# Causal products of a slot-attention kernel in blocks of 64 tokens instead of 128

## The chip, the cores and the metric

The kernel runs on one core of a Trainium2 chip. The time is the device time of one execution in microseconds. A core has five engines with a queue of their own each: TensorE (PE, with its weight loads listed as PEld), VectorE (DVE), ScalarE (ACT), GpSimd (POOL) and SyncE (SP, which here only starts DMAs). Each works through its queue in order, and semaphores make one wait for another. TensorE writes to PSUM, and ScalarE and VectorE take the results from there to SBUF.

## The reference, cut to what matters

Four sequences of 512 tokens, 512 wide, go through a layer norm, an attention with 64 slots per head, a second layer norm and a feed-forward part. The change touches the attention alone. It has 16 heads; q, k and s are 64 wide, v is 128 wide. In short, for each head:

```
z = cumlogsumexp(s) over the tokens
hk[t] = hk[t-1] * exp(z[t-1] - z[t]) + k[t] (x) exp(s[t] - z[t])     # 64 x 64
pv[t] = softmax(scale * q[t] . hk[t])                                # 64 slots
hv[t] = hv[t-1] * exp(z[t-1] - z[t]) + exp(s[t] - z[t]) (x) v[t]     # 64 x 128
o[t]  = pv[t] . hv[t]
```

With e = exp(s) and 1/z' as the inverse of e's running sum, both recurrences become sums over the past: the score of slot m at time t is (sum over u <= t of (q[t].k[u]) e[u,m]) / z'[t,m], and the output is the sum over u <= t of ((pv[t]/z'[t]) . e[u]) v[u]. Then o is normalised per head, multiplied by a weight and by silu of a gate, and projected by Wo.

## The kernel before, in words

A unit of work is a pair of heads (g, 8 of them) of one sequence (b, 4 of them): 32 units, in the order g over two sequences, then g over the other two. Keys, queries and e of the two heads lie on the two halves of the 128 partitions, transposed (feature by token). The 512 tokens are cut into NT = 4 blocks of 128. Sums over the past are done in two parts: products within a block, with a triangular mask, and products with a state, the sum over all earlier blocks. All these products are in float32. The projections are in float32r.

The parts of a unit that the change touches, with the lines of the profile:

- `diagonal_blocks` (from L607) makes, for each block and head, a 128x128 product out of 64 rows (L622), and VectorE multiplies it by the mask `tri` (L626, 128x512 per head). It is called by `query_key` (ps_a, from kT and qT) and `weight_slot` (ps_b, from eT and the weights wT).
- `states` (L636) makes the contributions of the first three blocks to the state of each head; `add_up` (L647, L649) has VectorE add them up in one copy and two adds. `key_states` calls it for keys and e (ps_sk, 64 wide), and GpSimd then copies the result into `sk_both` (L713), where both heads stand on a diagonal of 128x128; `value_states` calls it for e and v (ps_sv, 128 wide).
- `slot_scores` adds state times query (L724) and e times the masked product (L731) in one PSUM bank, and VectorE multiplies by 1/z' (okT, L739).
- `softmax` turns okT (ps_okn, L604), takes the maximum (mx, L746) and subtracts it (ok, L748); `softmax_exp` is on ScalarE (L753); `slot_weights` turns the result back (ps_w) and multiplies by 1/z' (wT, L770).
- `read_states` (L784) and `read_within` (L797) add the two parts of the output in PSUM (ps_ov). ScalarE squares it (L807), VectorE sums the squares (L808), and GpSimd raises to the power -0.5 (L812).

The order of all instructions is written out by hand in `attention`, engine by engine in program order; nothing reorders it. The output projection of the unit before (`before.project_output`, L883) is cut into pieces that stand between the steps of this unit's softmax: two of its matmuls before `softmax`, the rest of its first 128 tokens after it, and so on. Its results use the three buffers of the pool `ps3`, main and mixed part one each. ScalarE takes the main part (y, L895), and `add_output` has VectorE subtract the mixed part (L900) and GpSimd start a DMA that adds y to `stream` in memory (L901). So the third piece, `project_output(2, count=2)`, needs a buffer that `add_output(0)` releases. Ahead of `slot_scores` stand `gate_silu` for both heads (L839) and `exp_and_log`, which loads ScalarE's function table (L904).

Units with even g also project the values of two pairs of heads (L587); units with odd g do not. `other`, `piece`, `small` and `next_step` put waiting work in between: splitting weights, rounding the feed-forward weights, layer norms of the next sequence.

Of the kernel before, what the change touches and what calls it, by code (L numbers as in the profile page):

```python
# [44 lines left out]
P = 128  # L45
# [4 lines left out]
def kernel(  # L50
# [59 lines left out]
    def bank(name, n=None):  # L110
# [8 lines left out]
    ident = const.tile([P, P], F32, tag="ident", name="ident")  # L119
    make_identity(nc, ident)  # L120

    tri = const.tile([P, P], F32, tag="tri", name="tri")
    nc.gpsimd.memset(tri, 1.0)
    nc.gpsimd.affine_select(
        out=tri,
        in_=tri,
        compare_op=ALU.is_ge,
        fill=0.0,
        base=0,
        pattern=[[1, P]],  # L130
        channel_multiplier=-1,
    )
# [3 lines left out]
    sk_both = const.tile([P, NT - 1, HM], F32, tag="sk_both", name="sk_both")  # L136
    nc.gpsimd.memset(sk_both, 0.0)
# [461 lines left out]
    def transpose_4(src, name, n_bank=None):  # L599

        pt = bank(name, n_bank).rearrange("p (n t) -> p n t", n=NT)
        for n in range(NT):
            s = src[:, n, :] if len(src.shape) == 3 else src[:, n * P : (n + 1) * P]
            nc.tensor.transpose(pt[:, n, :], s, ident)  # L604
        return pt

    def diagonal_blocks(lT, rT, name):  # L607

        if name[0] == "a":
            pa = [ps2.tile([P, T], F32, tag="acc", name=f"ps_{name}_{h}") for h in range(HG)]  # L610
        else:
            pa = []
            for h in range(HG):
                if turn[0] in held:
                    turn[0] = (turn[0] + 1) % 3
                pa.append(bank(f"ps_{name}_{h}"))
        pa = [p.rearrange("p (n t) -> p n t", n=NT) for p in pa]
        for n in range(NT):
            cols = slice(n * P, (n + 1) * P)
            for h in range(HG):  # L620
                rows = slice(h * M, (h + 1) * M)
                nc.tensor.matmul(pa[h][:, n, :], lT[rows, cols], rT[rows, cols], start=True, stop=True)  # L622
        blocks = []
        for h in range(HG):
            a = one.tile([P, NT, P], F32, tag=f"a{h}", name=f"{name}_{h}")
            nc.vector.tensor_tensor(a, pa[h], tri.unsqueeze(1).to_broadcast([P, NT, P]), ALU.mult)  # L626
            blocks.append(a)
        return blocks

    def states(left, right, right0, width, name):  # L630


        pt = bank(name)[:, : (NT - 1) * width].rearrange("p (n w) -> p n w", w=width)
        for n in range(NT - 1):
            for h in range(HG):
                nc.tensor.matmul(  # L636
                    pt[h * M : (h + 1) * M, n, :],
                    left[:, n, h * M : (h + 1) * M],
                    right[:, n, right0 + h * width : right0 + (h + 1) * width],
                    start=True,  # L640
                    stop=True,
                )
        return pt

    def add_up(state, pt):

        nc.vector.tensor_copy(state[:, 0, :], pt[:, 0, :])  # L647
        for n in range(1, NT - 1):
            nc.vector.tensor_tensor(state[:, n, :], pt[:, n, :], state[:, n - 1, :], ALU.add)  # L649
# [3 lines left out]
    class Heads:  # L653
# [53 lines left out]
        def key_states(self):  # L707
            pt = states(self.kn, self.e, 0, M, f"ps_sk_{self.u}")
            self.sk = one.tile([P, NT - 1, M], F32, tag="sk", name=f"sk_{self.u}")
            add_up(self.sk, pt)  # L710
            for h in range(HG):
                rows = slice(h * M, (h + 1) * M)
                nc.gpsimd.tensor_copy(sk_both[rows, :, h * M : (h + 1) * M], self.sk[rows])  # L713
# [4 lines left out]
        def slot_scores(self):  # L718


            pok = ps2.tile([P, T], F32, tag="acc", name=f"ps_ok_{self.u}")
            for n in range(1, NT):
                cols = slice(n * P, (n + 1) * P)
                nc.tensor.matmul(  # L724
                    pok[:, cols], sk_both[:, n - 1, :], self.qT[:, cols],
                    start=(n == 1), stop=False,
                )
            for n in range(NT):
                for h in range(HG):
                    rows = slice(h * M, (h + 1) * M)  # L730
                    nc.tensor.matmul(  # L731
                        pok[rows, n * P : (n + 1) * P],
                        self.e[:, n, rows],
                        self.a[h][:, n, :],
                        start=False,
                        stop=(n == NT - 1),
                    )
            self.okT = one.tile([P, T], F32, tag="kn", name=f"okT_{self.u}")
            nc.vector.tensor_tensor(self.okT, pok, self.rzT, ALU.mult)  # L739
# [16 lines left out]
        def softmax_sum(self):  # L756
            nc.vector.tensor_reduce(self.sm, self.ok, AX.X, ALU.add)
            nc.vector.scalar_tensor_tensor(self.sm, self.sm, EPS, self.sm, ALU.mult, ALU.mult)

        def value_states(self):  # L760
            pt = states(self.e, both_v[self.b], self.v0, DV, f"ps_sv_{self.u}")
            self.sv = one.tile([P, NT - 1, DV], F32, tag="sv", name=f"sv_{self.u}")
            add_up(self.sv, pt)
# [11 lines left out]
        def read_states(self):  # L775
# [5 lines left out]
            for n in range(1, NT):  # L781
                for h in range(HG):
                    rows = slice(h * M, (h + 1) * M)
                    nc.tensor.matmul(  # L784
                        po[h][:, n, :],
                        self.wT[rows, n * P : (n + 1) * P],
                        self.sv[rows, n - 1, :],
                        start=(n == 1),
                        stop=False,
                    )  # L790

        def read_within(self):

            po = self.po
            for h in range(HG):
                for n in range(NT):
                    nc.tensor.matmul(  # L797
                        po[h][:, n, :],
                        self.bb[h][:, n, :],
                        both_v[self.b][:, n, self.v0 + h * DV : self.v0 + (h + 1) * DV],  # L800
                        start=False,
                        stop=(n == NT - 1),
                    )
            self.og = one.tile([P, HG, NT, DV], F32, tag="og", name=f"og_{self.u}")
            rs = two.tile([P, HG, NT], F32, tag="rs", name=f"rs_{self.u}")
            for h in range(HG):
# [3 lines left out]
                rs, rs, 1.0 / DV, self.sm.rearrange("p (n h) -> p h n", h=HG), ALU.mult, ALU.add  # L810
# [30 lines left out]
        def turn_output(self, h, n_bank=None):  # L841
# [3 lines left out]
            pt = transpose_4(self.og[:, h], f"ps_oT_{self.u}_{h}", n_bank)  # L845
# [60 lines left out]
    def first_unit():  # L906
# [27 lines left out]
        X.key_states()  # L934
        X.inverse()
# [19 lines left out]
        X.slot_weights()  # L955
        next_step()
# [12 lines left out]
    def attention(g, b, before, load, gated):  # L969
# [36 lines left out]
        if even:  # L1006
# [6 lines left out]
            if first or b > 1:  # L1013
                other(1)
            X.values(1)
# [4 lines left out]
            X.key_states()  # L1020
            X.inverse()
            X.query_key()
# [9 lines left out]
        else:  # L1032
# [6 lines left out]
            X.key_states()  # L1039
            if b > 1:  # L1040
# [36 lines left out]
        before.project_output(1)  # L1077
        before.project_output(2, count=2)
        X.slot_weights()
        if even and b == 1 and not first and not turned():  # L1080
# [5 lines left out]
        before.add_output(1)  # L1086
        next_step()
        before.project_output(2, True)
        before.add_output(2)
        X.weight_slot()  # L1090
        small()
        X.read_states()
        before.project_output(3)
        load("o")
        before.add_output(3)
# [33 lines left out]
    def ffn_hidden(b, c):  # L1129
# [8 lines left out]
        h = one.tile([P, T], F32, tag=("a0", "a1")[c % 2], name=f"h_{u}")  # L1138
# [231 lines left out]
```

## Time and profile before

| | us |
|---|---|
| three runs | 1456.4, 1457.46 (median), 1457.69 |
| the profiled execution | 1456.78 |
| its span, first to last instruction | 1455.1 |

| line, engine | what | count | mean ns |
|---|---|---|---|
| L622 PE | ps_a, 64 rows, 128 columns | 512 | 285 |
| L636 PE | ps_sk, 64 columns | 384 | 230 |
| L636 PE | ps_sv, 128 columns | 384 | 273 |
| L724 PE | ps_ok from states | 192 | 274 |
| L731 PE | ps_ok within a block | 512 | 279 |
| L784 PE | ps_ov from states | 384 | 275 |
| L797 PE | ps_ov within a block | 512 | 275 |
| L626 DVE | masks of ps_a, of ps_b, 128x512 | 64, 64 | 681, 683 |
| L649 DVE | adds of ps_sk, of ps_sv | 64, 64 | 225, 292 |
| L700 ACT | copy of 128x512 out of PSUM | 32 | 579 |
| L904 ACT | table load | 33 | 1283 |
| L713 POOL | copy of 64x192 into sk_both | 64 | 679 |

The trace lists two matmul records for each float32 matmul of the code: ps_a has 8 matmuls per unit, 16 records. The mean of a record is its time through the array; records follow each other closer than that. A row of the timeline merges records that follow each other, and gives the start, the length to the end of the last, the engine, line and operation, output and inputs, and the number. Where a unit's phases are compared, starts are subtracted.

### The profile page before, as it was taken

What the parts mean: (1) busy time and instruction counts of PE and PEld (TensorE: products, weight loads), DVE (VectorE), ACT (ScalarE), POOL (GpSimd) and SP (SyncE); (2) the same over time, 40 slices, a digit from 0 to 9 for tenths busy, and PEclk for the clock granted to TensorE, in tenths of its full rate; (3) what the DMA queues carried; (4) which work ended last, traced back from release to release, by engine and by line L of the source; (5) the groups of instructions that cost most, each with busy time, mean ns of one, the idle gap of its engine ahead of it and who ended that gap; (6) DMA issues with size and microseconds to landing.
All of it is one profiled execution on the core that took longest, in us unless ns stands there. A gap on an engine that the chain in (4) does not pass through costs nothing.

```text
span 1455.1 us, 22778 instructions
## 1 busy us (share of the span) xinstructions
PE 1430.3 (98%) x8875; PEld 1176.3 (81%) x8875; DVE 1101.0 (76%) x1968; ACT 705.8 (49%) x1215; POOL 242.3 (17%) x271
## 2 busy tenths in 40 slices
PE   8999999999999999999999999999999899999998
PEld 4777888888888887888888888888888788888886
DVE  7888868986888788878888888898888863435333
ACT  4655555555565555555545454456445442222221
POOL 3012111211121122211211121111212111000000
PEclk9999999999999999999999999999999999999999
DMA  8274556564656464456546654666465562101000
GB/s 333 96 208 138 182 160 173 175 209 139 174 174 208 111 232 123 138 152 196 160 110 186 211 167 106 190 205 195 110 181 167 145 181 29 59 1 58 0 30 29
DMA packets 80859, 212.51 MB, mean 146 GB/s; under 512 B 6168, under 2 KB 35120, under 8 KB 75568
## 3 DMA queue, kind: packets, MB, share of 16 engines
q1 hardware_dynamic: 62224, 177.49, 33.0%
q0 software_dynamic: 18528, 33.58, 15.5%
q8 instruction: 70, 1.15, 0.3%
q14 instruction: 37, 0.30, 0.1%
HBM read 107.23 MB, written 108.00 MB: 148 GB/s over the span
## 4 chain that ended last, share of the span: by engine, by line
PE 86%; DVE 7%; ACT 3%; issue 2%; POOL 1%; DMA 0%; SPq 0%; POOLq 0%; DVEq 0%
PE ps_o L883 8%; PE ps_g L528 8%; PE ps_v L587 8%; PE ps_fg L1118 6%; PE ps_fu L1118 6%; PE ps_g_m L551 4%; PE ps_v_m L587 4%; PE ps_o_m L883 4%; PE ps_fd L1179 3%; PE ps_ov L797 3%; PE ps_fe L1179 3%; PE ps_s L528 3%; PE ps_k L528 3%; PE ps_q L528 2%; PE ps_a L622 2%; PE ps_ok L731 2%
## 5 line engine op out<-in xcount | busy, mean ns | idle before, releaser
L901 POOL DMA_DIRECT2D stream<-y x128 | 113.7, 950 | 517.0 <-DVE y L900 514.3
L883 PE MATMUL ps_o<-w_o,oT 128*128 128x512 f32 x512 | 163.3, 421 | 0.0
L895 ACT ACTIVATE y<-ps_o 128x512 f32<-128x512 f32 x128 | 75.9, 593 | 127.8 <-PE ps_o L883 127.4
L528 PE MATMUL ps_g<-xs,w_g 128*128 128x512 f32 x496 | 125.0, 394 | 0.0
L587 PE MATMUL ps_v<-w_v,xs 128*128 128x512 f32 x480 | 122.4, 397 | 0.2 <-DVE qT L555 0.2
L1139 DVE SCALAR_TENSOR_TENSOR h<-ps_fu,scol,act 128x512 f32<-128x512 f32 x48 | 36.0, 750 | 112.8 <-PE ps_fu L1118 110.3
L528 PEld LDWEIGHTS ps_g<-xs,w_g 128*128 128x128 f32 x496 | 91.7, 188 | 19.5
L883 PEld LDWEIGHTS ps_o<-w_o,oT 128*128 128x128 f32 x512 | 84.8, 190 | 25.2 <-DVE y L900 7.0
L587 PEld LDWEIGHTS ps_v<-w_v,xs 128*128 128x128 f32 x480 | 87.7, 188 | 19.4 <-DVE qT L555 0.6
L713 POOL COPY sk_both<-sk 64x192 f32<-64x192 f32 x64 | 43.5, 679 | 331.2 <-DVE sk L649 329.3
L1118 PE MATMUL ps_fg<-xs,wf 128*128 128x512 f32 x384 | 95.6, 391 | 0.0
L1118 PE MATMUL ps_fu<-xs,wf 128*128 128x512 f32 x384 | 94.9, 389 | 0.0
L900 DVE TENSOR_TENSOR y<-y,ps_o_m 128x512 f32<-128x512 f32 x128 | 84.6, 680 | 6.1 <-ACT y L895 6.1
L1118 PEld LDWEIGHTS ps_fu<-xs,wf 128*128 128x128 f32 x384 | 72.1, 188 | 15.0
L1118 PEld LDWEIGHTS ps_fg<-xs,wf 128*128 128x128 f32 x384 | 71.6, 188 | 14.6
L595 ACT ACTIVATE v<-ps_v 128x512 f32<-128x512 f32 x60 | 35.9, 599 | 96.9 <-PE ps_v L587 96.9
L883 PE MATMUL ps_o_m<-w_o,oT 128*128 128x512 f32 x256 | 80.8, 397 | 0.1
L1145 ACT CAST both<-h 128x512 fp32r<-128x512 f32 x48 | 29.8, 620 | 95.3 <-DVE h L1139 95.3
L1136 ACT ACTIVATE act<-ps_fg,scol 128x512 f32<-128x512 f32 x48 | 33.0, 688 | 87.3 <-PE ps_fg L1118 87.3
L596 DVE TENSOR_TENSOR v<-v,ps_v_m 128x512 f32<-128x512 f32 x60 | 41.1, 684 | 43.6 <-PE ps_v_m L587 43.6
L812 POOL TENSOR_TENSOR rs<-rs,mhalf 128x8 f32<-128x8 f32 x32 | 58.8, 1839 | 78.8 <-DVE rs L809 54.6
L533 ACT ACTIVATE sg<-ps_g 128x512 f32<-128x512 f32 x62 | 36.9, 595 | 71.0 <-PE ps_g L528 39.7
(171 smaller groups left out, 3304.6 us busy)
## 6 DMA issues: line engine op xcount, KB each, us to landing
stream<-y POOLq DMA_DIRECT2D x128, 256.0 KB, 5.5
split_v<-w_v SPq DMA_DIRECT2D x4, 3072.0 KB, 11.6
split_g<-w_g SPq DMA_DIRECT2D x8, 1536.0 KB, 7.2
split_o<-w_o SPq DMA_DIRECT2D x8, 1536.0 KB, 6.2
w_v<-split_v SPq DMA_DIRECT2D x4, 3072.0 KB, 15.9
w_g<-split_g SPq DMA_DIRECT2D x8, 1536.0 KB, 6.5
w_o<-split_o SPq DMA_DIRECT2D x8, 1536.0 KB, 9.9
rounded<-qw SPq DMA_DIRECT2D x36, 256.0 KB, 3.6
```

The lines of the kernel that those rows point to most:

```text
L528: nc.tensor.matmul(self.p, products(self.nm, c, self.col0, i), xs[self.b][i][:, c, :], start=(i == 0 and c == 0), stop=(i == 1 and c == KC ...
L551: nc.tensor.matmul(self.m, products(self.nm, c, self.col0, 2), xs[self.b][2][:, c, :], start=(c == 0), stop=(c == KC - 1),)
L587: nc.tensor.matmul(dst, xs[b][i][:, c, n * P : (n + 1) * P], wt["v"][:, i, c * 2 * HV : (c + 1) * 2 * HV], start=(i == which[0] and c == 0 ...
L713: nc.gpsimd.tensor_copy(sk_both[rows, :, h * M : (h + 1) * M], self.sk[rows])
L797: nc.tensor.matmul(po[h][:, n, :], self.bb[h][:, n, :], both_v[self.b][:, n, self.v0 + h * DV : self.v0 + (h + 1) * DV], start=False, stop ...
L812: nc.gpsimd.tensor_tensor(rs, rs, mhalf.rearrange("p (h n) -> p h n", h=HG), ALU.pow)
L883: nc.tensor.matmul(dst, self.oT[:, i, h, n * P : (n + 1) * P], wt["o"][:, i, h * D : (h + 1) * D], start=(i in (0, 2) and h == 0), stop=(i ...
L895: nc.scalar.mul(y, p, 1.0 + DELTA)
L900: nc.vector.tensor_tensor(y, y, m, ALU.subtract)
L901: nc.gpsimd.dma_start(stream[self.b][n * P : (n + 1) * P, :], y, accum_op=ALU.add)
L1118: nc.tensor.matmul(pp, w[:, c * P : (c + 1) * P], xs[b][k][:, c, :], start=(c == 0 and k == 0), stop=(c == KC - 1 and k == 1),)
L1179: nc.tensor.matmul(sums[n], parts[k][:, n * P : (n + 1) * P], fw[c][2], start=(c == 0 and k == 0), stop=(c == NFC - 1 and k == 1),)
```

## The change

Blocks become 64 tokens. Each 128-token block n now has two halves, sub = 0 and 1, and every product is 64 rows by 64 columns of the array, so it lies in one quarter of it; which one follows from the partitions of its inputs and of its output. Consecutive matmuls go to different quarters. The products above the diagonal blocks of 64 are no longer made.

- `diagonal_blocks`: 16 matmuls with 64 moving columns instead of 8 with 128; the masks cover 128x256 instead of 128x512.
- `states`: 14 matmuls into two PSUM banks (even and odd halves) instead of 6 into one. `add_up`: ScalarE copies the even sums, VectorE adds the odd ones to that copy, then adds up in SBUF.
- Matmuls of a quarter need their inputs on given partitions. So GpSimd makes moved and completed copies of the key states and of the value states (one copy and two adds; two copies and two adds), ScalarE moves halves of the queries (`move_queries`) and of the weights (`move_weights`), two copies each. `sk_both` and its copies go.
- `slot_scores`: 14 and 16 matmuls into two banks instead of 3 and 8 into one; okT in two VectorE multiplications of 128x256. `read_states` and `read_within`: 14 and 16 matmuls instead of 6 and 8.
- `softmax_sum`: the square of sm moves from VectorE to three small ScalarE activations. The second head's output has its halves crossed, which is undone in its transposes by a crossed identity.
- Order in `attention`: in even units, `query_key` and `key_states` come ahead of `values(1)`; `move_queries` stands after `key_states`, `move_weights` ahead of `weight_slot`; `add_output(1)` comes ahead of `project_output(2, count=2)`, the third piece's end ahead of the work that is put in between, and `project_output(3)` ahead of `read_states`.
- In the feed-forward part the buffers of h change from `a0`, `a1` (now smaller) to `eT`, `rzT`.

```diff
     def diagonal_blocks(lT, rT, name):
...
+            pa.append(p[:, : NT * SB].rearrange("p (n t) -> p n t", n=NT))
         for n in range(NT):
-            cols = slice(n * P, (n + 1) * P)
-            for h in range(HG):
-                rows = slice(h * M, (h + 1) * M)
-                nc.tensor.matmul(pa[h][:, n, :], lT[rows, cols], rT[rows, cols], start=True, stop=True)
+            for sub in range(2):
+                c = half(2 * n + sub)
+                for h in range(HG):
+                    nc.tensor.matmul(
+                        pa[h][half(sub), n, :], lT[half(h), c], rT[half(h), c], start=True, stop=True
+                    )
...
-    def add_up(state, pt):
-
-        nc.vector.tensor_copy(state[:, 0, :], pt[:, 0, :])
+    def add_up(own, pts, state):
+
+        nc.scalar.copy(own, pts[0])
+        nc.vector.tensor_tensor(state, pts[1][:, : NT - 1, :], own[:, : NT - 1, :], ALU.add)
         for n in range(1, NT - 1):
-            nc.vector.tensor_tensor(state[:, n, :], pt[:, n, :], state[:, n - 1, :], ALU.add)
+            nc.vector.tensor_tensor(state[:, n, :], state[:, n, :], state[:, n - 1, :], ALU.add)
...
         def key_states(self):
...
+            add_up(own, pts, sk[:, 1:, :])
...
+            nc.gpsimd.tensor_copy(states_moved[half(0), 1:, :], sk[half(1), 1:, :])
+            nc.gpsimd.tensor_tensor(states_moved[half(1)], own[half(0)], sk[half(0)], ALU.add)
+            nc.gpsimd.tensor_tensor(own[half(1)], own[half(1)], sk[half(1)], ALU.add)
+
+        def move_queries(self):
+            qT = self.qT.rearrange("p (n s t) -> p n s t", s=2, t=SB)
+            for sub in range(2):
+                nc.scalar.copy(self.moved[half(sub), 1], qT[half(1 - sub), :, sub, :])
...
         def value_states(self):
...
+            add_up(svo, pts, self.sv)
+            self.moved_v = moved = one.tile([P, NT, DV], F32, tag="kT", name=f"moved_v_{self.u}")
+            nc.gpsimd.tensor_copy(moved[half(0), 1:, :], self.sv[half(1)])
+            nc.gpsimd.tensor_copy(moved[half(1), 0, :], svo[half(0), 0, :])
+            nc.gpsimd.tensor_tensor(moved[half(1), 1:, :], svo[half(0), 1:, :], self.sv[half(0)], ALU.add)
+            nc.gpsimd.tensor_tensor(svo[half(1), 1:, :], svo[half(1), 1:, :], self.sv[half(1)], ALU.add)
...
         X.softmax_exp()
         before.add_output(0)
         before.project_output(1)
+        before.add_output(1)
         before.project_output(2, count=2)
         X.slot_weights()
+        next_step()
+        before.project_output(2, True)
+        before.add_output(2)
...
-        before.add_output(1)
-        next_step()
-        before.project_output(2, True)
-        before.add_output(2)
+        X.move_weights()
         X.weight_slot()
         small()
-        X.read_states()
         before.project_output(3)
         load("o")
+        X.read_states()
```

## The prediction

> **What bounds the kernel.** I read the totals and the chain first, then what the weight loads of TensorE wait for, then one unit in order of time. A record is one MATMUL of the trace; a float32 matmul of the code leaves two, a transpose or a float32r matmul one.
>
> ```profile
> PE 1430.3 (98%) x8875; PEld 1176.3 (81%) x8875; DVE 1101.0 (76%) x1968; ACT 705.8 (49%) x1215; POOL 242.3 (17%) x271
> PE 86%; DVE 7%; ACT 3%; issue 2%; POOL 1%; DMA 0%; SPq 0%; POOLq 0%; DVEq 0%
> ```
>
> TensorE sets the end: busy for 98%, 86% of the chain, granted clock 0.998. So a nanosecond less on PE is worth one only as long as nothing that PE waits for is late. Where that cover is nil already, the waits of the weight loads show (total us, times, longest):
>
> ```profile
> PEld ps_o L883 <- DVE y L900: 7.0, 31, 0.4
> ```
>
> This line decides the forecast. In each of the 31 units that project a predecessor's output, one weight load of ps_o waits 0.23 us for `add_output(0)`. It still hides beside the running matmul, but nothing is left over. One unit on PE (start, length, records; the first three lines are from the even unit before):
>
> ```profile
> 655.23 0.57 PE L636 MATMUL ps_sk<-e,kn 128*64 128x64 f32 x12
> 655.73 1.16 PE L622 MATMUL ps_a<-qT,kT 64*128 64x128 f32 x16
> 656.82 2.11 PE L587 MATMUL ps_v<-w_v,xs 128*128 128x512 f32 x8
> ...
> 667.84 0.83 PE L724 MATMUL ps_ok<-qT,sk_both 128*128 128x128 f32 x6
> 668.60 1.09 PE L731 MATMUL ps_ok<-a,e 128*64 128x128 f32 x16
> 670.28 0.73 PE L883 MATMUL ps_o<-w_o,oT 128*128 128x512 f32 x2
> ...
> 673.61 0.66 PE L883 MATMUL ps_o<-w_o,oT 128*128 128x512 f32 x2
> ...
> 675.58 1.16 PE L622 MATMUL ps_b<-wT,eT 64*128 64x128 f32 x16
> ...
> 677.34 1.19 PE L883 MATMUL ps_o<-w_o,oT 128*128 128x512 f32 x4
> ...
> 678.84 1.95 PE L797 MATMUL ps_ov<-v,b 128*128 128x128 f32 x16
> 680.54 2.08 PE L528 MATMUL ps_s<-xs,w_s 128*128 128x512 f32 x8
> ```
>
> Starts count, not lengths, since records overlap. ScalarE and VectorE in the same stretch:
>
> ```profile
> 669.12 1.15 ACT L839 ACTIVATE sg<-sg 128x512 f32<-128x512 f32 x2
> 670.28 1.28 ACT L904 ACT_TABLE_LOAD   x1
> ```
>
> ```profile
> 670.39 0.29 DVE L647 COPY sv<-ps_sv 128x128 f32<-128x128 f32 x1
> 670.72 0.62 DVE L649 TENSOR_TENSOR sv<-ps_sv,sv 128x128 f32<-128x128 f32 x2
> 671.48 0.69 DVE L746 TENSOR_REDUCE mx<-ps_okn 128x8 f32<-128x512 f32 x1
> ...
> 672.82 0.68 DVE L900 TENSOR_TENSOR y<-y,ps_o_m 128x512 f32<-128x512 f32 x1
> ```
>
> ScalarE is shut in two silus and a table load until 671.56, while VectorE adds up the value states by itself, runs the softmax and ends `add_output(0)` at 673.50. PE starts the third ps_o at 673.61.
>
> **What the change takes from PE.** L797 uses the whole array: 16 records in 1.70 us, 106 ns each. In the groups on half tiles the single records start in twos, about 7 ns apart, and the next two follow after 106 to 109 ns with 128 moving columns (L622, L731) and after 58 ns with 64 (ps_sk, L636). So two tiles run at once and the moving columns set the pace. The trace shows no four tiles at once. I take four to run as two do: four records per 58 ns, or per 109 ns with 128 columns. Leaving and entering a tile shape costs too: ps_sk and ps_a take 1.59 us against 6x58 + 8x106 = 1.20, so 0.39 for two changes; L731 with ps_sv takes 1.68 against 14x109 = 1.53, 0.15 for one. I take 0.2 per change, and 0.1 for an entry that becomes new (the last group before 655.23 leaves such a gap).
>
> Keys: 16+14 matmuls, 60 records, 15 rounds of 58 = 0.87, with a change 1.07, was 1.59: **-0.52**.
> Weights and reading: ps_b 8 rounds of 58 and a change = 0.66; ps_ov 14+16 matmuls, 15 rounds of 109 and a change = 1.84; as project_output(3) now parts the two, one entry more, 0.1: 2.60. Before, 675.58 to 677.34 and 678.84 to 680.54, 3.46: **-0.86**.
> Scores and value states: 15 rounds of 58, 7 of 109, change and entry, about 1.88, was 670.28 - 667.84 = 2.44: 0.56 less, but see the wait.
> All three times 32 units would be 62 us, to 1395 us.
>
> **What the change puts on the path.** `add_up` now starts with a ScalarE copy of the even sums. In program order it stands behind the silus and the table load, and these hang on the gate projection, which the change doesn't touch: the copy starts at 671.56 however early PE is. It takes 0.58 (L700, the same shape out of PSUM): 672.14. VectorE's 128x384 add waits for it: between 0.29 (128 columns, L649) and 0.68 (512), 0.55 in a straight line, 672.72 with a handover of 0.03. Two adds of 128x128 follow at 0.29 each and 0.03 for their dependence: 673.36. Only then come mx, ok and the add of L900, which wait behind it in VectorE's queue; mx starts at 673.3, not 671.48: **+1.83**. ps_o at 673.61 needs the buffer that this L900 frees, so it starts at 675.44. The 0.56 from the scores vanishes into this wait; counted from the gate, PE is 1.83 later. Bounds: with the adds at the 0.225 of 64 columns and the wide one at 0.45 it is 1.6; with 0.68 and 0.60 for wide add and copy 2.0.
>
> **The rest, per unit.** The masks of L626 halve: 4x0.68 to 4x0.42; okT becomes two of 0.42; VectorE has about 0.6 less in sum, off the path. ScalarE gets two copies of 128x512 and 128x256 (0.58, 0.37), four of 64x256 (0.37, the 128x256 row; 128 columns and 512 bound it at 0.3 and 0.6) and three tiny squares: about 3 us more, at 49% busy; the query moves have over 6 us of gate products as cover, the weight moves the 2 us of ps_o and ps_b. GpSimd trades two 64x192 copies (0.68 each) for seven operations of 128 to 384 columns, by that row and the 1.29 us of 128x512 (L1163) some 5.6 us. The value moves start at 673.4, end by about 677 and are needed at the moved read_states, 1.5 us of ps_o after ps_b, about 679.5; stream's DMAs wait behind them in GpSimd's queue by up to 3 us, and they are needed some units later. Without this cover read_states would wait, us for us.
>
> GpSimd beside VectorE: of the 64 adds of L856, with both inputs in SBUF, the 31 that overlap a copy of L713 take 757 ns, the others 684. I take nothing for that, as mx, ok and y run before the moves. [...]
>
> PE is earlier against VectorE elsewhere too; waits that it has today without cover (ps_kn 5.9, ps_xn 4.6, ps_b 5.0 us in all) grow. The bounds are 0 and the whole 1.38 saved; I take **+0.30**, near the 0.5 per unit that they cost today.
>
> **Sum.** 1.83 - 0.52 - 0.86 + 0.30 = +0.75 us, times 31 is +23; the first unit, which has no output to project, gains 1.4: +22. The profiled execution took 1456.8 (span 1455.1), the median is 1457.5: **1479 us**. With 1.6 and nothing late, +0.22 a unit, 1462; with 2.0 and 0.6, 1494.
>
> **Rivals.**
> A, faster: the delay at the third ps_o is smaller. It is the place, the price is up to 1.83 a unit, and it decides at 1.38, the saving outside; a copy that got past the table load, or a ps_o with cover there, gives 0.6 or less: 1.38 - 0.6 = 0.78 x 31, 1432; without any delay 1395. For it: PE has 98%. Against: the 31 waits above and a fixed queue order.
> B, more slower: four tiles start no faster than the mean of the two-tile row, 29 ns a record (58/2): rounds of 116, in 23 rounds of 64 columns +1.33 and in 15 of 128 +0.10 a unit: +44, 1523. For: no row has a shorter mean. Against: 7 ns between neighbours. [...]
> C: the change does not do what it says, two tiles at a time as before. Rounds double: 23x58 + 15x109 = 2.97 a unit, +92, 1571. For: nothing in the trace shows four. Against: both row halves and column halves do overlap.
>
> **How the numbers follow.** Forecast 0.60 (1462 to 1500), B 0.20 (1500 to 1525), C 0.05, A 0.10, no change 0.05. 0.2%, 2.9 us, is about what a measurement can tell from no change. Slower 0.85, same 0.05, faster 0.10. The range 1456 to 1518 takes in forecast, no change and most of B.
>
> **To be checked.** Right, if PE waits for y (L952 there) at ps_o 31 times for some 2 us, if svo's copy follows the table load at once, and ps_a with ps_sk takes 1.1 us. Wrong, if that wait is below 1 us, if ps_a's 32 records spread over more than 0.7 us, or if read_states waits for GpSimd.

## The result, and the profile after

The changed kernel takes 1537.15 us (median of 4 runs, 1534.98 to 1537.49) against 1457.58: a ratio of 1.054, interval 1.0521 to 1.0558. The direction was forecast, the size was not: +80 us against +22, and outside the range. The profiled execution took 1537.05, with a span of 1535.3.

The page's totals and its chain by engine:

```profile
PE 1426.9 (93%) x13163; PEld 1124.3 (73%) x13163; DVE 1095.2 (71%) x1968; ACT 798.4 (52%) x1503; POOL 358.5 (23%) x433
...
PE 51%; DVE 26%; ACT 15%; issue 6%; DMA 1%; POOL 1%; DVEq 0%; ACTq 0%; POOLq 0%
```

TensorE is busy for almost as many microseconds as before, in a span that is 80 us longer, and its share of the chain fell from 86% to 51%. VectorE and ScalarE took that share, although VectorE's busy time hardly moved. That points to the order of the work rather than to its amount. The waits (engine, line, what it waited for: total us, times, longest):

```profile
DVE sv L662 <- ACT svo L661: 73.4, 31, 3.0
...
ACT sq L792 <- DVE sm L788: 64.2, 31, 2.8
...
PE ps_o L935 <- DVE y L952: 58.0, 29, 2.0
```

The first and the last are the forecast delay. The middle one is a wait that did not exist before and that the prediction did not name. One unit on TensorE (the first three lines are from its values, the rest from the scores on):

```profile
701.39 0.69 PE L629 MATMUL ps_a<-qT,kT 64*64 64x64 f32 x32
701.91 0.64 PE L650 MATMUL ps_sk<-e,kn 64*64 64x64 f32 x28
702.48 2.11 PE L591 MATMUL ps_v<-w_v,xs 128*128 128x512 f32 x8
...
717.20 0.27 PE L756 MATMUL ps_ok<-moved 64*64 64x64 f32 x1
...
719.05 0.73 PE L935 MATMUL ps_o<-w_o,oT 128*128 128x512 f32 x2
...
724.71 0.73 PE L935 MATMUL ps_o<-w_o,oT 128*128 128x512 f32 x2 [2.00 <-DVE y L952]
...
726.73 0.69 PE L629 MATMUL ps_b<-wT,eT 64*64 64x64 f32 x32
727.35 1.21 PE L935 MATMUL ps_o<-w_o,oT 128*128 128x512 f32 x4
...
728.95 0.32 PE L839 MATMUL ps_ov<-moved_v,moved_w 64*64 64x128 f32 x1
...
730.85 2.11 PE L532 MATMUL ps_s<-xs,w_s 128*128 128x512 f32 x8
```

Keys take 702.48 - 701.39 = 1.09 us, scores and value states 719.05 - 717.20 = 1.85. ps_b takes 0.62, ps_ov 1.90, and the third ps_o starts after a wait of 2.00. ScalarE and VectorE around that wait:

```profile
719.54 1.28 ACT L956 ACT_TABLE_LOAD   x1
720.83 0.59 ACT L661 COPY svo<-ps_sv 128x512 f32<-128x512 f32 x1
```

```profile
721.45 0.56 DVE L662 TENSOR_TENSOR sv<-ps_sv,svo 128x384 f32<-128x384 f32 x1 [2.39 <-ACT svo L661]
...
723.98 0.68 DVE L952 TENSOR_TENSOR y<-y,ps_o_m 128x512 f32<-128x512 f32 x1
```

From the end of the table load to the third ps_o it is 724.71 - 720.82 = 3.89 us, before 673.61 - 671.56 = 2.05. That is +1.84, and +1.83 was forecast.

A second thing is new. The mean granted clock is 0.972, before 0.998. Three neighbouring stretches of the changed kernel (span of the stretch; its length; busy time of PE, PEld, DVE, ACT, POOL; then PEclk, the granted clock):

```profile
515.44:518.85 3.41, 1.41 (x9) 1.00 (x8) 2.71 (x5) 1.12 (x2) 2.91 (x5) 0.99 0.00 0
518.85:522.27 3.42, 3.42 (x39) 2.36 (x38) 2.04 (x5) 1.40 (x3) 2.18 (x3) 0.51 0.69 86
522.27:525.68 3.41, 3.41 (x68) 2.70 (x67) 1.45 (x3) 1.21 (x4) 1.09 (x2) 1.00 0.97 143
```

In the first, TensorE works for 1.41 us and is idle for 2.00, the wait at ps_o. In the second it gets half the clock, and makes 39 matmul records where the third makes 68. The trace has 24 such stretches of 3.413 us after the start of the program, the kernel before has one (each has one more at the very end).

### The profile page after: what moved, and what is told of

Its sections match the earlier page's. It is cut to its first block, busy times and chain, and to the rows that moved or that the text cites. A ratio compares the mean times of both kernels' runs of the same rounds, so it can differ in the third digit from the quotient of the medians.

```text
span 1535.3 us, 32075 instructions
## 1 busy us (share of the span) xinstructions
PE 1426.9 (93%) x13163; PEld 1124.3 (73%) x13163; DVE 1095.2 (71%) x1968; ACT 798.4 (52%) x1503; POOL 358.5 (23%) x433
## 4 chain that ended last, share of the span: by engine, by line
PE 51%; DVE 26%; ACT 15%; issue 6%; DMA 1%; POOL 1%; DVEq 0%; ACTq 0%; POOLq 0%
PE ps_fg L1175 6%; PE ps_fu L1175 6%; PE ps_v L591 6%; PE ps_o L935 5%; PE ps_fd L1236 3%; PE ps_fe L1236 3%; PE ps_v_m L591 3%; ACT L956 3%; PE ps_g L532 2%; ACT L891 2%; DVE y L952 2%; DVE oT L908 2%; DVE oT L909 2%; PE ps_o_m L935 2%; PE ps_s L532 2%
## 5 line engine op out<-in xcount | busy, mean ns | idle before, releaser
L935 PE MATMUL ps_o<-w_o,oT 128*128 128x512 f32 x512 | 179.5, 455 | 58.0 <-DVE y L952 58.0
L935 PEld LDWEIGHTS ps_o<-w_o,oT 128*128 128x128 f32 x512 | 92.5, 206 | 88.4 <-DVE y L952 70.7
L804 POOL COPY moved_v<-sv 64x384 f32<-64x384 f32 x32 | 16.0, 499 | 380.1 <-PE ps_o_m L935 343.2
L591 PEld LDWEIGHTS ps_v<-w_v,xs 128*128 128x128 f32 x480 | 86.7, 188 | 17.2
L935 PE MATMUL ps_o_m<-w_o,oT 128*128 128x512 f32 x256 | 90.9, 439 | 4.9 <-ACT y L947 4.9
L728 POOL COPY moved<-sk 64x192 f32<-64x192 f32 x32 | 15.9, 497 | 284.3 <-DVE sk L664 284.3
L935 PEld LDWEIGHTS ps_o_m<-w_o,oT 128*128 128x128 f32 x256 | 51.3, 209 | 26.7 <-ACT y L947 15.8
L662 DVE TENSOR_TENSOR sv<-ps_sv,svo 128x384 f32<-128x384 f32 x32 | 17.8, 557 | 73.4 <-ACT svo L661 73.4
```

The costliest lines, as they stand in the source:

```text
L591: nc.tensor.matmul(dst, xs[b][i][:, c, n * P : (n + 1) * P], wt["v"][:, i, c * 2 * HV : (c + 1) * 2 * HV], start=(i == which[0] and c == 0 ...
L935: nc.tensor.matmul(dst, self.oT[:, i, h, n * P : (n + 1) * P], wt["o"][:, i, h * D : (h + 1) * D], start=(i in (0, 2) and h == 0), stop=(i ...
```

## The experiments

**First question: is it the wait at ps_o, and does the half clock come from the wait or from the small tiles?**

*fill14* keeps TensorE busy in the wait:

```diff
+        idle = ps2.tile([P, T], F32, tag="acc", name=f"ps_fill_{X.u}")
+        for _ in range(14):
+            nc.tensor.transpose(idle[:, :P], ident, ident)
         before.project_output(2, count=2)
```

> The changed kernel with 14 more transposes of the identity, into a PSUM tile that nobody reads, ahead of the third piece of the output projection, where PE waits 2.0 us for add_output(0). They add 14 x 107 ns = 1.5 us of work inside that wait and move nothing else. Theory 1 (the half clock is set off by the wait): the third ps_o starts as late as before, some 0.5 us of the wait are left, most of the 20 half-clock stretches that follow such a wait go, 20 x 1.7 us = 34 us less: about 1503 us, granted clock 0.99 or more. Theory 2 (the quarter-array matmuls count as little work and set it off, the wait is incidental): clock stays at 0.972, 1537 us.

Measured: 1519.78 us, ratio 1.0428 (1.0411 to 1.0446). The clock is back at 0.995, with 4 half-clock stretches in place of 24. So idleness sets them off, and not the shape of the tiles. But only 17 us came back, half of what was expected:

```profile
PE ps_o L935 <- DVE y L952: 13.3, 28, 0.5
```

The dummies keep TensorE busy for 52 us, and 13 us of waiting are left behind them; from the end of the product ahead of them to the third ps_o it is 60 us in all, about the 58 of the wait that they fill. Apart from the dummies TensorE is busy for 1399 us, 27 less than in the changed kernel, and its other waits are 7 us longer. So the stretches had cost TensorE less than the 34 us that were expected, and a part came back as waiting elsewhere. Some 62 us of the loss remain at almost full clock.

*late_table* lets svo's copy run ahead of the table load:

```diff
-        exp_and_log()
         X.slot_scores()
         X.value_states()
+        exp_and_log()
```

> The changed kernel with the load of ScalarE's table after value_states instead of ahead of slot_scores, so that the copy of the even value sums runs between the silus and the table load, 1.28 us earlier. Theory 1: the wait at the third ps_o falls from 2.0 to about 0.75 us (31 x 1.25 = 39 us), and with so short a wait the half-clock stretches go too (34 us): about 1464 us, clock above 0.99. Theory 2: 39 us less only, 1498 us, clock 0.97. If the copy is not what delays the softmax: no change.

Measured: 1470.67 us, ratio 1.0089 (1.0074 to 1.0104), 7 us above the 1464 of theory 1; 17.2 us of waits at ps_o, none above 0.6, and 4 stretches at half clock.

*sums_late* keeps the copy where it is, and moves VectorE's value sums and GpSimd's value moves, as a step `value_sums` of their own, behind the first output's subtraction:

```diff
...
         before.add_output(0)
+        X.value_sums()
         before.project_output(1)
```

> The changed kernel with VectorE's three adds of the value states, and GpSimd's moves, after add_output(0) instead of ahead of softmax, so the ScalarE copy is no longer on the way to the softmax. Theory 1: the wait at the third ps_o falls below 0.3 us, 60 us less, and about 35 us of half clock: 1440 to 1450 us, clock 0.99 or more, a new wait of up to 0.4 us at ps_b or ps_ov allowed for, as the adds then stand ahead of wT and the moves start later. Theory 2: 1475 us, clock 0.97.

Measured: 1464.3 us, ratio 1.0044 (1.0028 to 1.0061). No wait for y at the third ps_o is left. The place and the mechanism of the forecast delay are shown: 73 of the 80 us go with it, the half clock included. But the time was expected at 1440 to 1450, so something else is late too.

*old_copy* is the other side: the kernel before, with nothing but this detour of the value states through ScalarE:

```diff
-            add_up(self.sv, pt)
+            own = one.tile([P, NT - 1, DV], F32, tag="ok", name=f"svo_{self.u}")
+            nc.scalar.copy(own, pt)
+            nc.vector.tensor_copy(self.sv, own)
+            for n in range(1, NT - 1):
+                nc.vector.tensor_tensor(self.sv[:, n, :], self.sv[:, n, :], self.sv[:, n - 1, :], ALU.add)
```

> The kernel before, with its 128-token blocks and half-array tiles, and one edit: in value_states ScalarE copies the sums out of PSUM (128x384), VectorE copies that and adds up in SBUF. So the old kernel gets the new chain and none of the new tiles. Copy from 671.56 to 672.05 on the clock of the unit shown, VectorE's copy 0.3 to 0.55, two adds 0.62: mx starts some 1.65 us later. Theory 1: 31 x 1.65 = 51 us, and with a wait of about 1.7 us 12 to 18 half-clock stretches, 20 to 30 us: 1525 to 1540 us, clock 0.975 to 0.985. Theory 2: 1508 us with the clock at 0.998.

Measured: 1507.25 us, ratio 1.0341 (1.0326 to 1.0357): the detour alone, with large products, costs 50 us. The wait sets off no half clock but at the one place where the kernel before has it too, and the clock is 0.998. By the expectation that speaks for theory 2, the small tiles; but the waits came out at 1.3 us on average, not 1.7:

```profile
PE ps_o L887 <- DVE y L904: 41.2, 31, 1.7
```

*old_copy_long* makes them longer:

```diff
-            nc.vector.tensor_copy(self.sv, own)
+            for _ in range(3):
+                nc.vector.tensor_copy(self.sv, own)
```

> The kernel before with the ScalarE copy of ps_sv as in the run old_copy (1507 us, waits of 1.33 us at ps_o that set off no half clock), and the DVE copy of 128x384 behind it three times in place of once, so that the wait at ps_o is about 1.1 us longer, some 2.4 us. Theory 1 (a stretch of half clock follows when TensorE is idle for about 1.87 us or more within one window of a fixed 3.413 us grid, whatever the tile size): 15 to 25 stretches at half clock, and 1550 to 1570. Theory 2 (half clock has to do with the small tiles): at most two stretches, and 1507 + 31 x 1.12 = 1542.

Measured: 1564.33 us, ratio 1.0732 (1.0713 to 1.0751), clock 0.971, 26 stretches at half clock:

```profile
PE ps_o L888 <- DVE y L905: 65.5, 31, 2.5
```

The kernel before, without a single small tile, falls into the same state as soon as its waits go from 1.3 us on average to 2.1.

**Second question: what takes the rest in sums_late?**

*sums_y1_late* is sums_late with the second output's subtraction back where the kernel before has it:

```diff
-        before.add_output(1)
         before.project_output(2, count=2)
         X.slot_weights()
+        before.add_output(1)
```

> The run sums_late (1464 us: value sums and moved value states put behind the subtraction of output block 0) with the subtraction of output block 1 put back behind the slot weights, as the kernel before has it, so that VectorE multiplies wT 0.7 us earlier. If the waits of ps_b for wT (6.7 us in 30 waits) are on the path, 1455 to 1460; if the time is set by other results that TensorE reaches too early, or by the buffer of the third ps_o, 1463 to 1475.

Measured: 1466.0 us, ratio 1.0061 (1.0046 to 1.0076). TensorE's waits of ps_b for wT fell from 6.7 us to 0.3, and the time did not, so they are not it.

*tiles_only* leaves TensorE the small products and takes everything away that they need beside them (the reading of the value states; the key states and queries likewise, and the copies themselves are deleted). *old_moves* adds GpSimd's moves and ScalarE's copies to the kernel before, where nobody reads them; shown are those of the weights:

```diff
-                    if h == sub:
-                        weights = self.wT[half(sub), half(c)]
-                        state = self.svo[half(sub), n, :] if sub else self.sv[half(sub), n - 1, :]
-                    else:
-                        weights, state = self.moved_w[half(sub), n, :], self.moved_v[half(sub), n, :]
+                    weights, state = self.wT[half(sub), half(c)], self.sv[half(sub), max(n - 1, 0), :]
```

```diff
+            for sub in range(2):
+                nc.scalar.copy(self.moved_w[half(sub)], wT[half(1 - sub), :, sub, :])
...
+        X.move_weights()
         X.weight_slot()
```

> The changed kernel with its 64x64 products on TensorE as they are, and without what they need beside them: no copy of ps_sv by ScalarE (DVE adds up straight from one PSUM bank, as before the change), no moved queries, weights, key or value states, one DVE operation in place of the three Squares. The products read unmoved tiles, so their values are wrong; their shapes and number are unchanged. The order of the steps is that of the changed kernel. TensorE's tile groups are 62 us shorter than before. Theory 1 (what eats the rest is the added work on ScalarE, GpSimd and VectorE): nearly all of the 62 us come out, 1395 to 1410. Theory 2 (the rest is results of VectorE and ScalarE that TensorE now reaches earlier, whatever was added): a third to two thirds of it is given back in short waits, 1420 to 1440, with waits of ps_kn for kT, ps_okn for okT and ps_q for eT as long as in the changed kernel.

> The kernel before with the added copies alone: two 64x256 copies each of queries and weights on ScalarE, and the GpSimd copies and adds for moved key and value states, at the places where the changed kernel has them; nobody reads them, and the 128-wide products are unchanged. Theory 1 (added work eats the rest): 20 to 45 us slower, 1478 to 1500. Theory 2 (TensorE comes too early): the old kernel's TensorE has slack enough to cover them, within 8 us, 1457 to 1465.

Measured: tiles_only 1406.29 us, ratio 0.9648 (0.9632 to 0.9663); old_moves 1461.24, ratio 1.0024 (1.0014 to 1.0035). The totals of tiles_only:

```profile
PE 1377.8 (98%) x13163; PEld 1103.8 (78%) x13163; DVE 1069.9 (76%) x2000; ACT 701.6 (50%) x1215; POOL 195.2 (14%) x209
```

TensorE is at 98% again. So the 62 us that the small products save on TensorE are there to be had, 51 of them at once: the theory that TensorE merely comes too early everywhere falls. And the moves cost 4 us where TensorE is long. In sums_late the moves cost, together with the Squares and the sums through ScalarE, 58 (1464 against 1406); the next runs tell how much of it is theirs.

Four versions of sums_late divide that work: *sl_unread* does all of it but reads none of its results, *sl_no_act* goes without `move_queries` and `move_weights`, *sl_no_pool* without the GpSimd operations, *sl_no_moves* without both. For sl_no_pool, for instance:

```diff
-            nc.gpsimd.tensor_copy(moved[half(0), 1:, :], self.sv[half(1)])
-            nc.gpsimd.tensor_copy(moved[half(1), 0, :], svo[half(0), 0, :])
-            nc.gpsimd.tensor_tensor(moved[half(1), 1:, :], svo[half(0), 1:, :], self.sv[half(0)], ALU.add)
-            nc.gpsimd.tensor_tensor(svo[half(1), 1:, :], svo[half(1), 1:, :], self.sv[half(1)], ALU.add)
...
-                        weights, state = self.moved_w[half(sub), n, :], self.moved_v[half(sub), n, :]
+                    state = self.sv[half(sub), max(n - 1, 0), :]
...
```

> The run sums_late (1464 us; tiles_only, without any copy, gave 1406) with every copy and addition made, but with TensorE reading unmoved states, queries and weights instead, so that it waits for no copy (the values of those products are wrong). Theory 1 (TensorE waits for the moved halves): back to 1410 to 1425. Theory 2 (the copies lengthen the queues of ScalarE and GpSimd, and the evictions and multiplications that stand in them come later to TensorE at every hand-over): it stays at 1450 to 1464.

> The run sums_late without the four ScalarE copies of queries and weights (4 x 0.41 us a unit); TensorE reads unmoved queries and weights, GpSimd's moved states are still made and read. Theory 2 with ScalarE as the crowded queue: 1430 to 1442, the waits of ps_q for eT, ps_o_m for y and ps_b for wT shorter. Theory 2 with GpSimd (its work beside VectorE's, and the wait of ps_ov for svo): 1455 to 1464.

> The run sums_late without the GpSimd copies and additions of key and value states (some 3.8 us a unit of GpSimd); TensorE reads unmoved states, the moved queries and weights are still made and read. If GpSimd's share matters (svo late at ps_ov: 9 us there, and VectorE rows longer beside it): 1445 to 1455; if it is ScalarE's copies alone: 1455 to 1464.

> The run sums_late without both, the ScalarE copies of queries and weights and all the GpSimd work; what stays of the added work are ScalarE's copies of ps_sk and ps_sv, the three Squares, and the place of the value sums. If the shares add up, its gain over sums_late is the sum of those of sl_no_act and sl_no_pool. By theory 2 1412 to 1425, since tiles_only gave 1406; 1440 or more would put the loss on the copies of the banks and the later sums.

| | us | ratio to the kernel before |
|---|---|---|
| sums_late | 1464.3 | 1.0044 (1.0028 to 1.0061) |
| sl_unread | 1465.87 | 1.0051 (1.0036 to 1.0066) |
| sl_no_act | 1463.07 | 1.0036 (1.0023 to 1.0050) |
| sl_no_pool | 1437.01 | 0.9857 (0.9841 to 0.9872) |
| sl_no_moves | 1434.51 | 0.9840 (0.9823 to 0.9856) |

Nobody waits for the moved halves to any effect (sl_unread), and ScalarE's four copies are worth 1 to 3 us. GpSimd's work, 5.3 us a unit in sums_late (the 3.8 of the expectation are what it adds to the copies that it replaces), is worth 27 us, more than its expectation allowed, although reading its results costs TensorE nothing. Together the moves are worth 30 us here, where they cost 4 in old_moves: what is free beside a slow TensorE need not be free beside a fast one. The traces lead to VectorE as the path. GpSimd's own queue is not it: its power of -0.5 starts 0.14 us after VectorE's sum in sums_late and 0.17 in sl_no_pool, and no wait of ScalarE for a buffer of y is put down to the DMAs that start later. VectorE's groups that split oT, two inputs in SBUF (busy us, mean ns), without and with GpSimd's work:

```profile
L899 DVE TENSOR_TENSOR oT<-sg,oT 128x512 fp32r<-128x512 f32 x64 | 43.8, 685 | 1.4 <-ACT oT L895 1.4
```

```profile
L915 DVE TENSOR_TENSOR oT<-sg,oT 128x512 fp32r<-128x512 f32 x64 | 52.6, 822 | 1.4 <-ACT oT L911 1.4
```

In single instructions, the 32 of these 64 that overlap a GpSimd operation take 960 ns on average, up to 1231, the others 684. Over all groups VectorE's overlapped instructions are 34 us longer in sums_late than the same ones elsewhere in the run, 1 us in sl_no_pool. The subtraction of y, with an operand in PSUM, does not show it: in the changed kernel 62 of these overlap a GpSimd operation and take 682 ns, the other 66 take 684.

That leaves 28 us between sl_no_moves and tiles_only. *tiles_late* is tiles_only with the value sums at the late place:

```diff
...
         before.add_output(0)
+        X.value_sums()
         before.project_output(1)
```

> The run tiles_only (1406 us: small products alone, no copies or moves, wrong values) with VectorE's value sums put behind the subtraction of output block 0, as in sums_late; nothing else is added. If the 28 us between sl_no_moves (1434.5) and tiles_only are the price of the later place: 1425 to 1435. If they are ScalarE's copies of the banks ps_sk and ps_sv: 1406 to 1412.

Measured: 1403.5 us, ratio 0.9624 (0.9608 to 0.9640). The place costs nothing. What is left is ScalarE's copies of two banks, with the wider first add that VectorE makes of them, or the Squares.

*whole* and *whole_keys* take the copies of the banks out of VectorE's way: sums over whole blocks by 128-row products in a bank of their own, as before the change, so that only the states of the first halves pass through ScalarE. whole does it for the values, whole_keys for the keys too.

```diff
-            pts = states(self.e, both_v[self.b], self.v0, DV, f"ps_sv_{self.u}")
+            pts = whole_and_first(self.e, both_v[self.b], self.v0, DV, f"ps_sv_{self.u}")
...
```

> The changed kernel with all its moved halves and right values, but the value states of whole 128-token blocks by 128-row products into a bank of their own, as before the change, and only those of the first 64 tokens by small ones: VectorE adds up straight from that bank at the early place, and ScalarE's copy of the other bank is no longer on the way to ps_o. TensorE pays some 0.3 us a unit (12 records of 128 rows for 12 of the 28 small ones; before 24.16 us and after 29.26 us of ps_sv in 31 to 32 units), 9 us. From tiles_only 1406 + 9 + 27 (GpSimd) + 2 (queries and weights) + 0 to 10 (copies of the banks): 1444 to 1454, faster than the kernel before, and no wait over 1 us at ps_o. If the wait at ps_o for the sums was only replaced by one for something else, 1460 or more.

> The run whole with the key states made in the same way. The sums of the keys wait for no ScalarE copy either, TensorE pays another 0.25 us a unit or 8 us. No tile waits for the key sums by the profile of the changed kernel, so 1450 to 1462, some 6 us above whole; below whole only if VectorE, which waits for that copy in its order, is on the path there.

Measured: whole 1460.18, ratio 1.0016 (1.0006 to 1.0026); whole_keys 1472.74, ratio 1.0101 (1.0086 to 1.0116), both above what was expected. The products cost more than I had worked out: over the run ps_sv takes 58.5 us from start to start, 29.3 in sums_late, so 29 more where 9 were expected. The products of the first halves alone start in twos, some 0.1 us apart, so they use only two of the four quarters at a time:

```profile
594.57 1.09 PE L683 MATMUL ps_sv<-v,e 64*64 64x128 f32 x16
```

For the keys the price buys nothing. ScalarE at the end of a unit of whole, and the next unit's ps_s on TensorE:

```profile
606.98 0.21 ACT L825 ACTIVATE sq<-sm 128x4 f32<-128x4 f32 x1 [2.41 <-DVE sm L821]
...
607.64 1.09 ACT L892 ACTIVATE og<-ps_ov 128x512 f32<-128x512 f32 x2
608.61 0.61 ACT L537 ACTIVATE eT<-ps_s 128x512 f32<-128x512 f32 x1
```

```profile
606.22 2.11 PE L532 MATMUL ps_s<-xs,w_s 128*128 128x512 f32 x8
```

Here the wait from the profile of after is seen at work. TensorE is done with ps_ov when it goes on to ps_s at 606.22, but ScalarE stands for 2.41 us until VectorE has the softmax sum, does three Squares of four columns, and squares ps_ov only at 607.64. VectorE's sums of these squares, the output's scale and the eviction of ps_s stand behind them. Moving the Squares behind the squares of ps_ov, and nothing else:

```diff
         def softmax_sum(self):
             nc.vector.tensor_reduce(self.sm, self.ok, AX.X, ALU.add)
-            nc.scalar.activation(self.sq[:, 0, :], sm[:, 0, :], AF.Square, scale=root)
...
                 nc.vector.tensor_reduce(rs[:, h, :], self.og[:, h], AX.X, ALU.add)
+            nc.scalar.activation(self.sq[:, 0, :], sm[:, 0, :], AF.Square, scale=root)
...
```

> The run whole (1460 us, all moved halves, right values) with the three Squares of the softmax sums put behind the squares of ps_ov on ScalarE, in place of ahead of them; nothing else is moved. If the wait of ScalarE for the softmax sum and its 0.62 us of Squares hold up the eviction of ps_s and with it VectorE's eT and the waits of ps_q for eT and ps_kn for kT: 1435 to 1450, faster than the kernel before, with these waits shorter. If the copies of the banks are the cause of the 28 us, or the chain rs to scale_output grows by what the other saves: 1457 to 1462.

> The run sums_late (1464 us) with the same move of the Squares. If they are the cause: 1440 to 1452; whole_sq has none of the waits of ps_b for wT that the later sums bring here (6.7 us), but pays 12 us for its longer states on TensorE, so that the two end within 8 us of each other.

> The changed kernel (1537 us) with only the three Squares of the softmax sums moved behind the squares of ps_ov on ScalarE. The wait at ps_o is counted from TensorE's own last product of the scores and values, so an earlier start of the unit moves its begin and its end alike: if the loss of the Squares is one of its own, it comes out in full, 1537 - 17 = 1520. If ps_o waits for ScalarE or VectorE work that runs through from the start of the unit, the wait grows by what is saved, and the time stays at 1532 to 1538.

| | with the Squares moved, us | without | ratio to the kernel before |
|---|---|---|---|
| whole_sq | 1443.24 | 1460.18 | 0.9909 (0.9893 to 0.9926) |
| sums_late_sq | 1447.57 | 1464.3 | 0.9931 (0.9918 to 0.9943) |
| squares_late (the changed kernel) | 1513.54 | 1537.15 | 1.0390 (1.0375 to 1.0405) |

Seventeen microseconds in two versions, 24 in the changed kernel, where 7 half-clock stretches go as well. Counted from the first record of ps_s (medians over the units), the squares of ps_ov start 1.43 us later in whole and 0.10 in whole_sq, the eviction of ps_s 2.40 and 2.15, and VectorE's subtraction that completes eT 4.88 and 4.20: VectorE's work behind the squares moves more than the eviction does. ScalarE's wait for sm is gone in whole_sq, and its page reads like that of a kernel bound by TensorE:

```profile
ACT sq L889 <- DVE sm L821: 1.8, 9, 0.2
```

```profile
PE 1412.6 (98%) x13163; PEld 1126.7 (78%) x13163; DVE 1087.2 (75%) x1968; ACT 798.2 (55%) x1503; POOL 357.9 (25%) x433
...
PE 86%; DVE 7%; ACT 3%; DMA 2%; issue 1%; POOL 0%; SPq 0%; DVEq 0%; ACTq 0%; POOLq 0%
```

whole_sq beats both kernels: 0.9% faster than before, and it leaves nothing of the work out.

## Why the prediction was wrong

**TensorE's part: right.** Keys 1.09 us (1.07 forecast), ps_b 0.62 (0.66), ps_ov 1.90 (1.84), scores and value states 1.85 (1.88; the terms named there add up to 1.93). From start to start the six tile groups lose 62 us over the run, and 62 were worked out. Records start four per 55 to 60 ns with 64 columns and per 110 with 128, as assumed, and within such a group of four neighbours start 7 ns apart, each in a quarter of its own; so rivals B and C are out. With the delay and all the added work out of the way rival A's 1395 is nearly reached (tiles_late 1403.5).

**The delay at the third ps_o: right.** +1.84 against +1.83, 29 waits of 2.00 us where 31 were forecast, and svo's copy follows the table load at once. old_copy prices it by itself at 50 us; late_table takes out most of it, sums_late all. The three marks that should show the forecast right were there, read_states did not wait for GpSimd, and the time was still 58 us off. The marks tested the steps that were named, not the sum.

**"PE is earlier against VectorE elsewhere too ... I take +0.30": this step failed.** It stood for everything that was not worked out, and it was priced by waits of the kernel before. Three mechanisms stand in its place:

- *The half clock was not considered.* The trace of before had the row, with one wait of 2.7 us at ps_b; its only stretch at half clock within the run, 3.4 us, begins 1.1 us after that wait's end:

```profile
PE ps_b L622 <- DVE y L900: 4.6, 2, 2.7
```

The forecast put a wait of 2 us into every unit, and none of its terms says what TensorE does after such a wait. fill14 prices it at 17 us.

- *"Three tiny squares" were counted as busy time.* Their 0.62 us a unit are off the path by length. But they left VectorE, where sm is made, for ScalarE, which has to wait for sm, and the prediction does not ask what stands behind them in ScalarE's order: the squares of ps_ov, on whose sums VectorE works next, and the eviction of ps_s. squares_late prices this at 24 us, some of it half clock.
- *"GpSimd beside VectorE: ... I take nothing for that."* The step looked at mx, ok and y, which read PSUM and are indeed not touched (683, 692 and 682 ns beside GpSimd in the changed kernel, 691, 692 and 680 without it in the kernel before). But the key moves run beside the split of oT, as L713's shorter copies did before, and the row of before was misread there (min/median/max of one in ns, first and last start in us):

```profile
L856 DVE TENSOR_TENSOR oT<-sg,oT x64: 678/684/831, 77.5 to 1193.4; 128x512 fp32r<-128x512 f32 x64
```

The 757 ns of the 31 overlapped ones is a mean of two cases. In 15 VectorE started first and took 681 ns; in 16 GpSimd's copy started first, and VectorE took 829 and ended 0.54 us after the copy. In the changed kernel it is the same, 0.55 us, but the operation that VectorE runs into is 1.07 us long instead of 0.69. So L908, L856 of before, takes some 1225 ns there, and 958 on average over its 32 overlapped ones. In the changed kernel VectorE's overlapped instructions are 19 us longer, 4 before; in sums_late they are 34 longer, and leaving GpSimd's work out is worth 27. What holds VectorE back there, beyond this order of the starts, no run shows.

By size: 17 + 24 + 15 to 27 is 56 to 68 us (15 is what VectorE's overlapped instructions gained in length, 19 less 4); the forecast had 9 for all of it and missed 58. The shares were measured in different versions, and the 24 include some of the 17, so that the sum fits is no proof that they add. Of the 28 us between sl_no_moves and tiles_only the Squares explain 17, as measured in two other versions; that the rest belongs to ScalarE's copies of the two banks and VectorE's longer first add is inferred, no run isolates it.

**The range.** Its upper end rested on rival B, a slower array. It held no term for a second new wait or for the clock, and no case in which two costs come on top of the forecast together.

## What to carry to other kernels

When the bounding engine is made faster, price the helpers' work by its place in each in-order queue, not by its length: a 0.2 us operation that waits for another engine (in whole the first Square, 0.21 us after 2.41 of waiting) holds up all that is queued behind it. Work that is hidden today can cost far more once its cover is gone (the moves 4 us in old_moves, 30 in sums_late), so measure the saving alone and the added work alone, as tiles_only and old_moves do, before tuning both together. Where a forecast puts a new idle stretch on TensorE, ask for the clock after it (here 19 of the 29 waits of 2.0 us were followed by 3.413 us at half clock). And before a difference of means is set aside, look whether a mean mixes two cases.

## What the hardware showed that was not expected

In the traces the half clock goes by a fixed grid. In each run the half-clock stretches, but for the one at the very end, are 3.413 us long (two of them twice that) and start at whole multiples of 3.413 us from one another. TensorE's idle time in each window of that grid, by its records, whose ends are modelled, told what came next. In the traces of the two kernels all 24 windows with more than 1.9 us idle were followed by a window at half clock, none of 842 with less than 1.75 us, and 1 of 5 between them; over 20 traces of this study 96 of 98, 5 of some 8400 and 11 of 23. So a wait of 2.0 us set it off where it fell into one window, and mostly not where the grid cut it: in the changed kernel the half clock followed all 15 waits at ps_o that fell into one window, and 4 of the 14 that were cut. The waits of old_copy, 1.3 us on average, did not set it off, and its clock stayed at 0.998. In these runs, then, 1.9 us idle out of 3.413, a little over half a window, were enough in nearly every case.

In the traces of the two kernels, the VectorE operations that take over 15 ns longer on average beside GpSimd have all their operands in SBUF: in the changed kernel 684 ns became 958 on average and 1231 at most for the 128x512 subtraction with two inputs that splits oT, while that of y, which reads PSUM, took 684 alone and 682 beside GpSimd. For the split of oT it went by who started first: where VectorE did, 15 times in each kernel, it took 681 ns before and 683 after, as if alone, and GpSimd's operation ended 0.20 us behind it.
